# Attention scores with a second level of Strassen's rule in four of seven products, and the next image's block sums at a later place

## The chip, the cores and the metric

The kernel runs on one core of one Trainium2 chip. The metric is device time in microseconds (us) of one execution. Before the change three runs gave 2621.7, 2623.08 and 2623.68 us, median 2623.08. One further execution was taken with the hardware profiler: 2621.26 us, of which 2619.2 us are the span of the trace and 2.06 us lie around it. The clock granted to TensorE was 1.00 of full speed in that execution.

The engines are named as the profile names them: PE (TensorE, matrix products; PEld is its weight load), ACT (ScalarE), DVE (VectorE), POOL (GpSimd), SP (SyncE, which only issues transfers here). PSUM is the memory that PE writes its results to.

## The reference

Two images x of 512 channels and 32 by 32 = 1024 positions go through a deformable attention block with an MLP (layer 0) and then through a plain attention block (layer 1). The change lies in layer 1 alone:

```python
q = xt @ Wq.T + bq          # xt: 1024 positions x 512 channels
k = xt @ Wk.T + bk
v = xt @ Wv.T + bv
attn = softmax(q @ k.T / sqrt(512))
out = (attn @ v) @ Wp.T + bp
return x + out.T
```

Everything is float32. The kernel folds the weights: with G from Wq and Wk, the scores are Q^T x, where Q = G x + bias has 512 channels by 1024 positions (what is constant along a softmax row is left out); and N from Wv and Wp replaces v and the last projection.

## The kernel before, in words

**Layer 1, per image b (the loop at L1192).** All products are multiplied by Strassen's rule (in Winograd's form): a 2 by 2 block matrix product takes seven block products instead of eight, numbered by `PARTS` (L104) with the weight block and the moving block that each takes. Sums of blocks, made by DVE (`fold`, `spread`, `plus`) or POOL, feed the products and combine the results. The stages of one image are, in PE's order:

1. *q stage* (L1224): seven products of G with x give Q in four quadrants `qs[0..3]` of 256 channels by 512 positions; `fold` (L1228) adds the three block sums `qs[4..6]` on DVE.
2. *scores* (`scores(u)`, L1248; u = 0, 1): for 512 query positions at a time, Q^T x against all 1024 positions. Each of the seven products is 256 queries x 512 keys over 256 channels: four `nc.tensor.matmul` calls, which the trace shows as 8 PE passes of 512 columns (two passes to a float32 call). The result quadrants c11, c12 (tile `e[0]`) and c21, c22 (`e[1]`) are filled by ACT copies and DVE additions out of PSUM. `softmax(e[1])` is traced after product 5 and `softmax(e[0])` after product 2, the last: a row maximum (DVE, L1235), a scale of it (L1236), two exponentials (ACT, L1239), a reciprocal (DVE, L1243), two multiplications (ACT, L1245).
3. *turn* (`turn(u)`, L1271): PE transposes the 512 x 1024 result into PSUM in four pieces of 8 passes, ACT copies each to `aT` (L1280), DVE makes two block sums (`spread`).
4. *v products* (`turned`, L1294): seven products of x with N, three of them between turn(0) and turn(1), four after.
5. *value stage* (from L1318): attn times v. Here four of the seven products (1, 6 in set 0; 7, 5 in set 1) are already split by a second level of the rule, by `twice` (L139); products 2, 3, 4 run whole (`plain`).

**`twice` (L139 to L180)** works on pairs of outer products ("sets"). Each set is seven inner steps in the order `STEPS` (L137): q = 1, 2, 6, 5, 7, 4, 3 at times 0, 1, 3, 4, 6, 9, 12; the second set starts 7 later; whole products and other work are slipped in at given times (`fills`). An order written out by hand holds for PE: every step is issued after the newest PE instruction. Steps 1, 6, 7 and 4 of a set pile up in one PSUM bank of a tile, and ACT copies the running sum out after each (lines 166, 170, 172, 176: d11, d12, d22, d21), so step 6 may start only when ACT has copied step 1, and so on. Steps 2, and 5 with 3, go to the two banks of a second tile; DVE adds step 2 to d11, step 5 to d22 and step 3 to d12. The MLP of layer 0 (`layer1`, L1057) uses the same function with inner blocks of 128 x 256 over 128 channels, each step being two calls, 4 passes of 256 columns.

**Order on the other engines.** Dependences and queue order are set by a scheduler at build time: an engine that comes free takes, of what is ready, the instruction that stands first in the program. The queue is then fixed, and each engine executes its own in order. `tc.issue_after` adds an edge behind an instruction of the same engine.

**PSUM** has four buffers of 128 x 1024 for these stages (`mq`, L1150), taken in rotation.

**`blocks(b)` (L925)** makes the three sums t1, t2, t3 (tile `tx`) and t4 of x that the q stage, the scores and the v products take as moving blocks: four DVE instructions, no transfers. For image 1 it is traced inside `second()` (L1416), the fill at time 6.5 of image 0's value stage, after `x_sums(1)` and `w_sums(1)`, and behind the newest DVE instruction.

Of the kernel before, what the change touches and what calls it, by code (L numbers as in the profile page):

```python
# [8 lines left out]
F32 = mybir.dt.float32  # L9
AF = mybir.ActivationFunctionType  # L10
ALU = mybir.AluOpType
# [3 lines left out]
P = 128  # L15
# [42 lines left out]
def conv_seq_kernel(ctx: ExitStack, tc: tile.TileContext, x, xt, kst, pst, cst, vec, wsm, outw, w1, w2, wl, wlt, brow, out):  # L58
    nc = tc.nc
# [52 lines left out]
    PARTS = {1: (0, 0), 2: (1, 2), 3: (6, 3), 4: (2, 6), 5: (4, 4), 6: (5, 5), 7: (3, 1)}  # L112
# [17 lines left out]
    def multiply(pool, order, product, took):  # L130
        for p in order:
            ps = pool.tile([P, 2, 512], F32, tag="ps2", name="sw")
            product(ps, *PARTS[p])
            took[p](ps)

    def plus(out, a, b_, op=ALU.add):
        nc.vector.tensor_tensor(out, a, b_, op)  # L137
# [44 lines left out]
    AT_W, AT_X = ((0, 0), (1, 0), (1, 1), (0, 1)), ((0, 0), (0, 1), (1, 0), (1, 1))  # L182
# [24 lines left out]
    with tc.tile_pool(name="lp", bufs=2) as lp:  # L207
# [37 lines left out]
        def load(b, k, wq=None):  # L245
# [367 lines left out]
        head, g, n = chain(0), weights(0), weights(1)  # L613
# [233 lines left out]
        for s in range(NS):  # L847
# [36 lines left out]
            if bg is None and s > ready and (s - ready) % 4 == 0 and (s - ready) // 4 <= 8:  # L884
                i = (s - ready) // 4 - 1
# [39 lines left out]
    def blocks(b):  # L925
        tx = xq.tile([P, 3, 2, 512], F32, tag="tx", name="tx")
        q = quarters(b)
        t1, t2, t3 = (tx[:, j] for j in range(3))
        t4 = f_pool.tile([P, 2, 512], F32, tag="sx", name="t4")
        nc.vector.tensor_tensor(t1, q[0], q[1], ALU.subtract)  # L930
        nc.vector.scalar_tensor_tensor(t2, t1, -1.0, q[3], ALU.mult, ALU.subtract)
        nc.vector.tensor_tensor(t3, q[3], q[1], ALU.subtract)
        nc.vector.scalar_tensor_tensor(t4, t2, -1.0, q[2], ALU.mult, ALU.subtract)
        return [q[0], t3, q[2], q[3], t1, t2, t4]

    with ExitStack() as top, tc.tile_pool(name="wp", bufs=1) as wp:
        halves = [(b, h) for b in range(B) for h in range(2)]
# [213 lines left out]
        for i, (b, p) in enumerate(units):  # L1151

            j, k = divmod(i, NCH)
# [37 lines left out]
    with tc.tile_pool(name="sp", bufs=1) as sp:  # L1191
        for b in range(B):  # L1192
# [27 lines left out]
            def q5(ps):  # L1220
                plus(q22, q22, ps)
                plus(q12, q12, ps)

            multiply(mq, (1, 6, 7, 4, 5, 3, 2), product(gg, xbl), {  # L1224
                1: q1, 6: lambda ps: plus(q12, q11, ps), 7: q7, 4: lambda ps: plus(q21, q22, ps), 5: q5,
                3: lambda ps: plus(q12, q12, ps), 2: lambda ps: plus(q11, q11, ps),
            })
            fold(nc.vector, [qs[:, j] for j in range(7)], ALU.subtract)  # L1228


            aT = sp.tile([P, 6, 4, 512], F32, name="aT")

            def softmax(e, sign):
                mx = sp.tile([P, 2], F32, name="mx1", bufs=4)
                nc.vector.tensor_reduce(mx, e, AX.X, ALU.max if sign > 0 else ALU.min)  # L1235
                nc.vector.tensor_scalar(mx, mx, -SC * sign, None, ALU.mult)  # L1236
                sm = sp.tile([P, 2], F32, name="sm1", bufs=4)
                for m in range(2):
                    nc.scalar.activation(  # L1239
                        e[:, m, :], e[:, m, :], AF.Exp, bias=mx[:, m : m + 1], scale=SC * sign,  # L1240
                        accum_out=sm[:, m : m + 1],
                    )
                nc.vector.reciprocal(sm, sm)  # L1243
                for m in range(2):
                    nc.scalar.activation(e[:, m, :], e[:, m, :], AF.Copy, scale=sm[:, m : m + 1])  # L1245


            def scores(u):  # L1248
                e = [sp.tile([P, 2, HW], F32, name=f"e{i}", bufs=2) for i in range(2)]
                c11, c12, c21, c22 = (e[i][:, :, n : n + 512] for i in range(2) for n in (0, 512))  # L1250

                def s7(ps):
                    plus(c22, c12, ps)
                    plus(c21, c22, c21, ALU.subtract)

                def s5(ps):
                    plus(c22, c22, ps)
                    plus(c12, c12, ps)
                    softmax(e[1], -1)

                def s2(ps):
                    plus(c11, c11, ps, ALU.subtract)
                    softmax(e[0], 1)

                multiply(mq, (4, 1, 6, 7, 5, 3, 2), product(qs, xbl, 256 * u), {
                    4: lambda ps: nc.scalar.copy(c21, ps), 1: lambda ps: nc.scalar.copy(c11, ps),
                    6: lambda ps: plus(c12, c11, ps), 7: s7, 5: s5, 3: lambda ps: plus(c12, c12, ps), 2: s2,
                })
                return e

            def turn(u, e):  # L1271
                for i in range(2):
                    for m in range(2):
                        ps = mq.tile([P, 2, 512], F32, tag="ps2", name="psx")
                        for c in range(8):
                            nc.tensor.transpose(  # L1276
                                ps[:, c // 4, c % 4 * P : (c % 4 + 1) * P], e[i][:, m, c * P : (c + 1) * P], ident
                            )
                        n = 256 * u + m * P
                        nc.scalar.copy(  # L1280
                            aT[:, i : i + 3 : 2, :, n : n + P],
                            ps.rearrange("p a (c n) -> p a c n", n=P),
                        )
                n = slice(256 * u, 256 * u + 256)
                spread([aT[:, j, :, n] for j in range(6)], range(2))

            e0 = scores(0)
            e1 = scores(1)
            turn(0, e0)
            vt = cp.tile([P, 7, 4, 256], F32, tag="big", name="vt")  # L1290
            vf = [vt[:, j].rearrange("p m n -> p (m n)") for j in range(7)]
# [23 lines left out]
            multiply(mq, (1, 6, 7), turned, took)  # L1315
            turn(1, e1)

            sets = ((1, 6), (7, 5))  # L1318
            where = {p: (g, e) for g, pair in enumerate(sets) for e, p in enumerate(pair)}
# [79 lines left out]
            def plain(p, took):  # L1399
                def go():  # L1400
                    ps = mq.tile([P, 2, 512], F32, tag="ps2", name="sw")
                    whole(ps, *PARTS[p])
                    took(ps)
                return go
# [9 lines left out]
                    spread([aT[:, j] for j in range(6)], (2,))  # L1414

            def second():  # L1416
                nonlocal xbl
                x_sums(1)
                w_sums(1)
                if b + 1 < B:  # L1420
                    with tc.issue_after(newest(mybir.EngineType.DVE)):
                        xbl = blocks(b + 1)
# [2 lines left out]
                (-1, plain(2, lambda ps: plus(x11, x11, ps))),  # L1425
                (-2, third),
                (6.5, second),
                (15, plain(3, lambda ps: plus(x12, x12, ps))),
                (20, plain(4, a4)),
            ), 1.0)  # L1430
# [116 lines left out]
```

## Time and profile before

| what | value |
|---|---|
| median of three runs | 2623.08 us |
| profiled execution, its span | 2621.26 us, 2619.2 us |
| q stage, image 0 / image 1 (PE) | 2313.96 to 2338.00 / 2464.46 to 2488.49 |
| scores(0), scores(1), image 1 | 2488.49 to 2512.53, 2512.53 to 2536.56 (24.04 us each) |
| turn(0), v products, turn(1), image 1 | 2536.56 to 2567.72 |
| value stage, image 0 | 2417.23 to 2464.46 (47.2 us) |
| value stage, image 1 | 2567.72 to 2613.04 (45.3 us) |
| DVE and ACT busy in scores(1), image 1 | 13.30 us and 10.71 us of 24.03 |

Times are read on the axis of the trace, in us from the start of the span. A timeline line gives the start, the length, the engine, the source line, the operation, output and inputs, and in brackets how long the engine was idle before it and what ended the wait. PE passes are pipelined: the length of a PE line includes the drain of its last pass, so the pace is read from one start to the next. L137 is the helper `plus`, L160 the products of `twice`, L1200 the whole products.

### The profile page before, as it was taken

The page shows a single profiled execution, that of the slowest core. Times are in us where ns is not written, and L with a number is a line of the kernel's source. Part 1 is how long each engine was busy: PE and PEld are TensorE (multiplying, and loading weights), DVE is VectorE, ACT ScalarE, POOL GpSimd, SP SyncE. Part 2 cuts the span into 40 slices and gives each one's busy share as a digit, 9 for nine tenths or more (in the row PEclk, how much of TensorE's full clock was granted, in tenths as well). Part 3 has the DMA queues.
Part 4 walks back from the last instruction along what each step waited for, and adds up shares of the span by engine and source line. Part 5 has one row for each costly group of instructions (what it writes and reads, how often), then busy time and mean ns, then how long its engine had stood idle before and what let it go on. Part 6 is the DMA issues. An engine that isn't in the chain of part 4 may idle for free.

```text
span 2619.2 us, 48156 instructions
## 1 busy us (share of the span) xinstructions
PE 2603.7 (99%) x19752; PEld 1030.5 (39%) x19752; DVE 2313.2 (88%) x1463; ACT 1750.4 (67%) x2325; POOL 814.1 (31%) x909
## 2 busy tenths in 40 slices
PE   9999999999999999999999999999999999999999
PEld 3333343333233233333333333334355655646556
DVE  7999999999999999999999999999786586666656
ACT  5887898878888887887887777777733242314041
POOL 1333333333333333333333333333332334200100
PEclk9999999999999999999999999999999999999999
DMA  5888878888887889787887878888777768400202
GB/s 189 178 174 184 184 172 171 183 180 196 173 176 169 180 171 205 172 180 169 181 183 164 182 172 178 173 185 177 147 209 172 150 150 166 87 17 1 73 0 57
DMA packets 167531, 407.74 MB, mean 156 GB/s; under 512 B 24944, under 2 KB 73216, under 8 KB 164624
## 3 DMA queue, kind: packets, MB, share of 16 engines
q0 software_dynamic: 100736, 259.43, 54.6%
q1 hardware_dynamic: 66144, 144.93, 15.8%
q8 instruction: 156, 2.56, 0.4%
q14 instruction: 63, 0.52, 0.1%
q10 hardware_dynamic: 432, 0.31, 0.0%
HBM read 82.15 MB, written 6.55 MB: 34 GB/s over the span
## 4 chain that ended last, share of the span: by engine, by line
PE 91%; DVE 4%; ACT 2%; issue 2%; DMA 1%; DVEq 0%; POOL 0%; ACTq 0%; POOLq 0%; SPq 0%
PE ps L698 63%; PE sw L1041 7%; PE sw L1200 7%; PE sw L160 6%; PE sw L988 2%; PE sw L1298 2%; PE sim L784 1%; PE psg L600 1%; DVE hm L137 1%; PE psx L1276 1%; ACT rx L707 1%; DVE ub L717 0%; DVE h L681 0%; PE pkv L534 0%; DVE oe L137 0%
## 5 line engine op out<-in xcount | busy, mean ns | idle before, releaser
L698 PE MATMUL ps<-h,cw 128*32 128x512 f32 x16384 | 1776.4, 592 | 4.2 <-ACT rx L707 3.1
L681 DVE CUSTOM_DVE_ANT_1 h<-ta,tb 128x4096 f32<-128x4096 f32 (+1 forms) x257 | 1130.9, 4401 | 29.5 <-PE ps L698 26.7
L698 PEld LDWEIGHTS ps<-h,cw 128*32 128x32 f32 x16384 | 549.0, 110 | 1195.8 <-issue 1123.4
L707 ACT ACTIVATE rx<-ps,sc 128x1024 f32<-128x1024 f32 x512 | 568.2, 1110 | 146.6 <-PE ps L698 125.2
L709 ACT ACTIVATE ub<-ps,sc 128x1024 f32<-128x1024 f32 x256 | 308.3, 1204 | 93.2 <-PE ps L698 93.0
L717 DVE SCALAR_TENSOR_TENSOR ub<-rx,sc,ub 128x1024 f32<-128x1024 f32 x256 | 326.8, 1276 | 6.6 <-ACT ub L709 6.6
L736 POOL DMA_DIRECT2D ua<-uc x126 | 154.4, 1235 | 319.5 <-DMA ua<-uc 312.7
L736 POOL DMA_DIRECT2D ua<-ua x189 | 219.4, 1306 | 26.0 <-DMA ua<-uo 19.1
L1041 PE MATMUL sw<-hm,w2t 128*128 128x512 f32 x448 | 193.9, 592 | 0.8 <-DVE hm L125 0.7
L719 POOL DMA_DIRECT2D uo<-ub x127 | 123.7, 974 | 221.7 <-DVE ub L717 207.0
L709 ACT ACTIVATE uo<-ps,sc 128x1024 f32<-128x1024 f32 x128 | 154.2, 1205 | 51.7 <-PE ps L698 51.4
L717 DVE SCALAR_TENSOR_TENSOR uo<-rx,sc,uo 128x1024 f32<-128x1024 f32 x128 | 163.5, 1278 | 8.2 <-ACT uo L709 8.2
L736 POOL DMA_DIRECT2D uc<-uo x63 | 53.1, 842 | 333.7 <-DMA uc<-uo 327.6
L1041 PEld LDWEIGHTS sw<-hm,w2t 128*128 128x128 f32 x448 | 84.9, 190 | 105.3 <-issue 98.2
L137 DVE TENSOR_TENSOR hm<-hm,sw 128x512 f32<-128x512 f32 (+1 forms) x80 | 58.7, 738 | 69.9 <-PE sw L160 50.4
L719 POOL DMA_DIRECT2D ua<-ub x64 | 58.4, 912 | 170.3 <-DVE ub L717 160.5
L661 ACT ACTIVATE ta<-fb,vs 128x512 f32<-128x512 f32 (+1 forms) x65 | 88.9, 1370 | 8.0 <-DMA fb<-fdr 8.0
L709 ACT ACTIVATE ua<-ps,sc 128x1024 f32<-128x1024 f32 x64 | 77.0, 1204 | 20.5 <-PE ps L698 20.1
L709 ACT ACTIVATE uc<-ps,sc 128x1024 f32<-128x1024 f32 x64 | 77.1, 1205 | 20.1 <-PE ps L698 17.7
L1364 POOL DMA_DIRECT2D xs<-rs x6 | 7.2, 1195 | 261.4 <-DVE rs L137 261.4
L166 ACT COPY hm<-sw 128x512 f32<-128x512 f32 x24 | 14.1, 587 | 111.2 <-PE sw L160 111.2
L717 DVE SCALAR_TENSOR_TENSOR uc<-rx,sc,uc 128x1024 f32<-128x1024 f32 x64 | 81.8, 1278 | 2.7 <-ACT uc L709 2.5
(294 smaller groups left out, 2659.5 us busy)
## 6 DMA issues: line engine op xcount, KB each, us to landing
uo<-ub POOLq DMA_DIRECT2D x127, 512.0 KB, 5.6
fb<-fdr SPq DMA_DIRECT2D x64, 512.0 KB, 5.1
ua<-ub POOLq DMA_DIRECT2D x64, 512.0 KB, 5.8
uc<-ub POOLq DMA_DIRECT2D x64, 512.0 KB, 5.2
ua<-ua POOLq DMA_DIRECT2D x63, 256.0 KB, 6.2
ua<-uo SPq DMA_DIRECT2D x63, 256.0 KB, 2.3
ua<-uo POOLq DMA_DIRECT2D x63, 256.0 KB, 6.0
uc<-uc POOLq DMA_DIRECT2D x63, 256.0 KB, 6.9
```

What stands on the lines that cost most here:

```text
L137: nc.vector.tensor_tensor(out, a, b_, op)
L160: nc.tensor.matmul(bank[:, e, :], w, x, start=(q in (1, 2, 5) and e == k == 0), stop=True, skip_group_check=True,)
L661: nc.scalar.activation(ta.rearrange("p j x -> p x j")[:, :, j0:j1], fb[:, 0, :, j0:j1], AF.Identity, bias=col("cb1"), scale=col("w1x"),)
L681: nc.vector._custom_dve(TENSOR_ADD_SAT, out=h1[:, y : y + step].rearrange("p y t x -> p (y t x)"), in0=a.unsqueeze(1).to_broadcast([P, ste ...
L698: nc.tensor.matmul(ps[32 * q : 32 * q + 32, h, :], cw2[:, 32 * z : 32 * z + 32], h1[:, 16 * h : 16 * h + 16, q, :], start=True, stop=True,)
L707: nc.scalar.activation(o, ps, AF.Relu, bias=sc[:, 4 + z : 5 + z])
L709: nc.scalar.activation(o, ps, AF.Relu, bias=sc[:, 4 + z : 5 + z], scale=sc[:, z : z + 1])
L717: nc.vector.scalar_tensor_tensor(r[1], r[0], sc[:, z : z + 1], r[1], ALU.mult, ALU.add)
L719: nc.gpsimd.dma_start(out=sums[s][1], in_=sums[s][3], accum_op=ALU.add)
L736: nc.gpsimd.dma_start(out=out, in_=in_, accum_op=ALU.add)
L1041: nc.tensor.matmul(ps[:, m, :], w[:, a, k, m * P : (m + 1) * P], x[:, b_, k, :], start=(k == 0), stop=(k == 1),)
L1200: nc.tensor.matmul(ps[:, m, :], w[:, a, k, c + m * P : c + (m + 1) * P], x[b_][:, k, :], start=(k == 0), stop=(k == nk - 1),)
```

## The change

It touches four places.

- **scores(u)** is rewritten on top of `twice`: products 1, 6 (set 0) and 7, 5 (set 1) are split into seven inner products each of 128 queries x 256 keys over 128 channels; products 4, 2 and 3 stay whole, as fills at times -1, 14 and 20. Set 0 accumulates straight into c11 and c12 of `e[0]`; set 1 into scratch r7, r5 (`qr`). `done(1)` combines and calls `softmax(e[1])`; product 3, the last, calls `softmax(e[0])`.
- **Sums for the inner products**: eight DVE instructions for the moving side (`qx`), traced before the q stage; four DVE and four POOL instructions for the weight side (`inner_q`), traced between and after the `fold` instructions.
- **A scratch tile `sw_`** of 48 KB per partition takes the place (tag) of `aT`; `aT` itself is taken only after scores(1), so it comes free for turn(0) when the last reader of `sw_` is done.
- **blocks(b+1)** moves from `second` (time 6.5) to a fill of its own at time 14, behind the newest DVE instruction there.

The diff, with all that matters of it:

```diff
-        return [q[0], t3, q[2], q[3], t1, t2, t4]
+        return [q[0], t3, q[2], q[3], t1, t2, t4, tx]
...
+            sets = ((1, 6), (7, 5))
+            where = {p: (g, e) for g, pair in enumerate(sets) for e, p in enumerate(pair)}
+            sw_ = sp.tile([P, 12, 1024], F32, tag="aT", name="sw_")
+            qx = sw_[:, 0:4, :].rearrange("p j (a n) -> p j a n", a=4)
+            qe = [sw_[:, n : n + 2, :].rearrange("p a (j e u n) -> p (a j) e u n", j=2, e=2, u=2) for n in (4, 6)]
+            qr = sw_[:, 8:10, :].rearrange("p e (m n) -> p e m n", m=2)
+            for t, blk in ((xbl[7][:, 0:3], slice(1, 4)), (xbl[0][:, None], slice(0, 1))):
+                x = [t[:, :, k, 256 * n : 256 * n + 256] for k, n in AT_X]
+                f, a, c, d = (qx[:, j, blk] for j in range(4))
+                plus(a, x[1], x[0], ALU.subtract)
+                plus(c, x[3], a, ALU.subtract)
+                plus(f, x[3], x[1], ALU.subtract)
+                plus(d, x[2], c, ALU.subtract)
             multiply(mq, (1, 6, 7, 4, 5, 3, 2), product(gg, xbl), {
...
-            fold(nc.vector, [qs[:, j] for j in range(7)], ALU.subtract)
-            aT = sp.tile([P, 6, 4, 512], F32, name="aT")
+            def inner_q(g):
...
+                engine = (nc.vector, nc.gpsimd)[g]
+                f, a, c, d = (qe[g][:, j] for j in range(4))
+                engine.tensor_tensor(a, w[3], w[2], ALU.add)
+                engine.tensor_tensor(c, a, w[0], ALU.subtract)
+                yield
+                engine.tensor_tensor(f, w[0], w[3], ALU.subtract)
+                engine.tensor_tensor(d, w[1], c, ALU.subtract)
+            first = inner_q(0)
+            for which in ((0, 1), (3,), (2,)):
+                fold(nc.vector, [qs[:, j] for j in range(7)], ALU.subtract, which)
+                next(first, None)
+            for _ in inner_q(1):
+                pass
...
             def scores(u):
...
-                multiply(mq, (4, 1, 6, 7, 5, 3, 2), product(qs, xbl, 256 * u), {
-                    4: lambda ps: nc.scalar.copy(c21, ps), 1: lambda ps: nc.scalar.copy(c11, ps),
-                    6: lambda ps: plus(c12, c11, ps), 7: s7, 5: s5, 3: lambda ps: plus(c12, c12, ps), 2: s2,
-                })
+                def dest(g, m, h):
+                    if g == 0:
+                        return e[0][:, m, :].rearrange("p (e h n) -> p h e n", e=2, h=2)[:, h]
+                    return qr[:, :, m, 256 * h : 256 * h + 256]
+                r7, r5 = (qr[:, i] for i in range(2))
+                def done(g):
+                    if g == 0:
+                        plus(c12, c12, c11)
+                    else:
+                        plus(r7, r7, c12)
+                        plus(c21, r7, c21, ALU.subtract)
+                        plus(c22, r7, r5)
+                        softmax(e[1], -1)
+                        plus(c12, c12, r5)
+                def p3(ps):
                     plus(c12, c12, ps)
+                    softmax(e[0], 1)
+                twice(mq, sets, weights, moving, dest, done, (
+                    (-1, plain(4, lambda ps: nc.scalar.copy(c21, ps))),
+                    (14, plain(2, lambda ps: plus(c11, c11, ps, ALU.subtract))),
+                    (20, plain(3, p3)),
+                ), 1.0)
                 return e
...
             e1 = scores(1)
+            aT = sp.tile([P, 6, 4, 512], F32, name="aT")
             turn(0, e0)
...
             def second():
-                nonlocal xbl
                 x_sums(1)
                 w_sums(1)
+            def next_blocks():
+                nonlocal xbl
                 if b + 1 < B:
                     with tc.issue_after(newest(mybir.EngineType.DVE)):
                         xbl = blocks(b + 1)
...
                 (6.5, second),
+                (14, next_blocks),
```

More of the change, by code (lines that the diff above doesn't have):

```diff
@@ L1227, in conv_seq_kernel @@
             })
-            fold(nc.vector, [qs[:, j] for j in range(7)], ALU.subtract)
-            aT = sp.tile([P, 6, 4, 512], F32, name="aT")
+            def inner_q(g):
+                w = [
+                    qs[:, (slice(0, 6, 5), slice(3, 5))[g], k, :].rearrange("p e (u n c) -> p n e u c", u=2, n=2)[:, n]
+                    for k, n in AT_W
+                ]
+                engine = (nc.vector, nc.gpsimd)[g]
[11 more added lines that the diff above has]
+                pass
             def softmax(e, sign):
@@ L1250, in scores, with plain, go @@
                 c11, c12, c21, c22 = (e[i][:, :, n : n + 512] for i in range(2) for n in (0, 512))
[L1252 to L1257, printed above, removed]
+                one = product(qs, xbl, 256 * u)
+                def plain(p, took):
+                    def go():
+                        ps = mq.tile([P, 2, 512], F32, tag="ps2", name="sw")
+                        one(ps, *PARTS[p])
+                        took(ps)
+                    return go
@@ new lines, in weights, with moving @@
+                def weights(p, j):
+                    g, e_ = where[p]
+                    a = PARTS[p][0]
+                    if j < 3:
+                        k, n = AT_W[j]
+                        n = 256 * u + P * n
+                        return [qs[:, a, k, n : n + P]]
+                    return [qe[g][:, j - 3, e_, u, :]]
+                def moving(p, j):
+                    b_ = PARTS[p][1]
+                    if j in (0, 2, 3):
+                        k, n = AT_X[j]
+                        return [xbl[b_][:, k, 256 * n : 256 * n + 256]]
+                    return [qx[:, max(j - 3, 0), {0: 0, 4: 1, 5: 2, 1: 3}[b_], :]]
@@ L1258, in s5 @@
+                def p3(ps):
                     plus(c12, c12, ps)
-                    softmax(e[1], -1)
-                def s2(ps):
-                    plus(c11, c11, ps, ALU.subtract)
                     softmax(e[0], 1)
-                multiply(mq, (4, 1, 6, 7, 5, 3, 2), product(qs, xbl, 256 * u), {
-                    4: lambda ps: nc.scalar.copy(c21, ps), 1: lambda ps: nc.scalar.copy(c11, ps),
-                    6: lambda ps: plus(c12, c11, ps), 7: s7, 5: s5, 3: lambda ps: plus(c12, c12, ps), 2: s2,
-                })
+                twice(mq, sets, weights, moving, dest, done, (
[3 more added lines that the diff above has]
+                ), 1.0)
@@ L1316, in conv_seq_kernel @@
             turn(1, e1)
-            sets = ((1, 6), (7, 5))
-            where = {p: (g, e) for g, pair in enumerate(sets) for e, p in enumerate(pair)}
             x45 = [sp.tile([P, 2, 2, 2, 256], F32, tag="e0", name="x45", bufs=2) for _ in sets]
```

## The prediction

> **What bounds the kernel now.** I read first the page's busy times (PE 2603.7 of 2619.2 us) and the chain that ended last (PE 91%), then the busy times by stage for image 1, from the q stage to the value stage:
>
> ```profile
> 2464.46:2488.49 24.03, 24.03 (x57) 10.64 (x56) 9.94 (x10) 1.27 (x2) 3.40 (x3) 1.00 0.17 66
> 2488.49:2512.53 24.04, 24.04 (x58) 10.64 (x57) 14.13 (x12) 2.91 (x3) 0.00 (x0) 1.00 0.00 0
> 2512.53:2536.56 24.03, 24.03 (x58) 10.59 (x56) 13.30 (x13) 10.71 (x15) 0.00 (x0) 1.00 0.00 1
> 2536.56:2567.72 31.16, 31.16 (x177) 28.22 (x176) 20.47 (x19) 18.52 (x24) 0.00 (x0) 1.00 0.00 1
> 2567.72:2613.04 45.32, 45.05 (x161) 30.13 (x159) 32.20 (x33) 6.70 (x10) 3.58 (x3) 1.00 0.23 47
> ```
>
> The columns are window, length, then busy time of PE, PEld, DVE, ACT, POOL. In both halves of the scores (lines 2 and 3) PE has no idle time, DVE works 14 of 24 us, and ACT's softmax of the first half falls into the second (10.71 against 2.91). So PE sets the time, and nothing on PE waits: less PE work gains, and any wait that arises costs in full.
>
> **PE work.** A whole product takes 3.434 us (24.04 / 7). The pace of 256-column passes is shown by the MLP's use of `twice`:
>
> ```profile
> 2038.83 2.12 PE L160 MATMUL sw<-xe,w1e 128*128 128x256 f32 x8
> 2040.79 2.75 PE L160 MATMUL sw<-xb,w1x 128*128 128x256 f32 x12
> 2043.38 1.03 PE L160 MATMUL sw<-xe,w1x 128*128 128x256 f32 x4
> ```
>
> Twelve passes in 2043.38 - 2040.79 = 2.59 us: 0.864 us per step of four. A half becomes 3 x 3.434 + 14 x 0.864 = 22.39 us, so 1.65 us less; four halves, **6.6 us less**.
>
> The weight load of one pass lasts 190 ns beside 216 ns of pass, and the two overlap in these rows. [...]
>
> **blocks(1) moved.** Its four instructions now stand before the addition that an inner product waits for. First DVE's timeline, then PE's, both image 0:
>
> ```profile
> 2440.12 1.22 DVE L931 SCALAR_TENSOR_TENSOR tx<-tx,xs 128x1024 f32<-128x1024 f32 x1
> 2441.26 0.68 DVE L137 TENSOR_TENSOR rs<-rs,sw 128x512 f32<-128x512 f32 x1
> ...
> 2455.38 1.22 DVE L137 TENSOR_TENSOR xs<-xs,sw 128x1024 f32<-128x1024 f32 x1 [5.01 <-DMA xs<-rs]
> ```
> ```profile
> 2429.71 1.99 PE L160 MATMUL sw<-x,oe 128*128 128x256 f32 x8 [0.27 <-DVE rs L137]
> ...
> 2441.99 1.99 PE L160 MATMUL sw<-x,oe 128*128 128x256 f32 x8 [1.65 <-DVE rs L137]
> ```
>
> At 2441.99 PE had waited 1.65 us. Image 0's value stage lasts 47.23 us, image 1's, which has no blocks, 45.32: **1.9 us gained**. At time 14 the four land in DVE's idle 5.01 us (4.6 us of work); PE wants them at 2464.46, 9 us later. They issue no transfer and pass no queue but DVE's.
>
> The same rows show a wait that matters below: **inner step 5 of a set starts only after DVE has added step 2** (2441.26 + 0.68 = 2441.94, PE at 2441.99), though they use different banks.
>
> **Added sums.** qx: 4 instructions of 768 elements and 4 of 256. By the pitches of 512 (0.60 us) and 1024 (1.13 us) I take 0.87 and 0.34: 5.3 us with the dependences; ends 2.4 and 6.9 us. Image 1: DVE idles 5.65 us from 2465.94 to 2471.59. Image 0: they follow the MLP's last addition (2321.36), and DVE idles 7.3 us in the four gaps of the q stage; the products wait for a buffer only four products (13.7 us) later. Cost nothing at either end. POOL's four sums: 1.26 to 2.14 us each by its `gn` rows; the third ends 3.8 to 6.4 us after start, against 8.5 us until PE wants it: nothing, and one for one beyond. DVE's weight sums are priced next.
>
> **Waits in the scores.** Per half DVE's work grows from 13.3 to some 16.9 us (six additions of 512 elements on top of seven of 1024 and two maxima) and ACT's from 10.7 to some 14 (eight copies of 512 in place of one of 1024); both fit into 22.4 us, but PE now waits for single ones. Product 4 of scores(0) starts at time 0. DVE's steps are 0.60 us (512 elements), 1.13 (1024) and 2.20 (maximum), with 0.12 more after a dependence; ACT's 0.49 to 0.59 (d copies), 1.15 (exponential), 1.05 (multiplication); PE's result reaches a reader after 0.25. Who goes first, where several are ready, is read here on ACT:
>
> ```profile
> 2519.20 1.14 ACT L1239 ACTIVATE e<-e,mx 128x1024 f32<-128x1024 f32 x1
> 2520.24 0.19 ACT L1239 ACTIVATION_READ_ACCUMULATOR e<-e,mx 128x1 f32 x1
> 2520.33 1.13 ACT L1239 ACTIVATE e<-e,mx 128x1024 f32<-128x1024 f32 x1
> 2521.37 0.19 ACT L1239 ACTIVATION_READ_ACCUMULATOR e<-e,mx 128x1 f32 x1
> 2521.46 0.99 ACT L1266 COPY e<-sw 128x1024 f32<-128x1024 f32 x1
> 2522.36 2.19 ACT L1245 ACTIVATE e<-e,sm 128x1024 f32<-128x1024 f32 x2
> ```
>
> The copy of scores(1)'s product 1 (its PE work ended at 2519.39) stands behind the second exponential of scores(0): the older instruction goes first. Today that is free, since PE has four buffers; after the change PE waits for each such copy.
>
> *First half.* DVE: q11 at 0.25, folds 1.51 and 2.64, a 3.77, f 4.37, c 4.97, fold 5.57, d 6.70, d11 addition 7.30 to 7.99. Step 6 (due 5.16) needs c: 5.81, a wait of 0.65. Step 5 (due 6.67) needs d11: 8.14, 1.47. Then PE runs through to 24.49.
>
> *Second half.* DVE still has, from 21.31, d12, r7, c12, c21, c22, product 3's addition (0.60 + 5 x 1.13 and a dependence), then two maxima from 27.69 to 32.09, two scales. The new d11 addition runs 32.33 to 33.02; step 5, due 30.59, starts at 33.17: **2.58** (and 0.08 ahead of step 6). ACT starts the exponentials at 32.29 and works through six of the softmax's eight instructions until 38.99; d22, whose product ended at 34.89, comes then; step 4, due 36.61, starts at 39.64: **3.02**. ACT's last two multiplications end at 41.58, then set 1's d11: its step 6, due 40.50, starts at 42.23: **1.73**. The half ends at 54.27.
>
> *Turn.* The same tail of DVE follows scores(1). ACT's first copy to `aT`, due 55.4, waits until 56.46 for the last reader of `sw_`; the fourth transposed piece needs product 3's buffer (added at 56.33 to 57.55): **0.82**. scores(1)'s exponentials start at 62.06, its last multiplications at 69.66; turn(1), due 68.94, starts at 70.82, and its second piece waits a little: **2.06**. In the value stage DVE catches up behind 6.87 us of product 2.
>
> Sum of waits per image: 0.65 + 1.47 + 0.08 + 2.58 + 3.02 + 1.73 + 0.82 + 2.06 = 12.41; less 3.30 of work: +9.1 us, two images +18.2. In image 0 the exponential's table load (1.28 us, idle today) delays the exponentials some 0.3. With -1.9: +16.6. From the profiled execution: 2621.26 + 16.6 = 2637.9. The runs shown lie 0.4 to 2.4 us above that execution, so about 1 us is added: **2639 us**.
>
> The largest wait is 3.0 us; the granted clock stayed 1.00 through one of 1.65 us, and I price no clock loss. [...]
>
> **Rivals.**
> 1. *Faster: the d copies and additions pass ahead of the old softmax.* Place: ACT's and DVE's queues in scores(1). For it: ACT has only 14 us of work in 22.4, and an MLP unit (2037.09 to 2059.11, 22.02 us) loses only 0.4 against 21 x 0.864 + 3.434 = 21.58. Against: the ACT rows above. Price: 0.5 us of waits per half and none in the turn, so (1.0 - 3.3) x 2 - 1.9 = -6.5: 2615, or 2616 with the 1 us. It is faster where an image's waits stay under 4.2 us, and measurably so under 1.6.
> 2. *Slower, but half:* the maximum of e[1] goes before the additions of c12 (it misses its turn by 0.1 us), so exponentials start over 2 us earlier and the burst splits. Waits some 8 per image, +4.7 each, -1.9: 2629.
> 3. *About the same:* rival 2's order and no waits in the turn, 5 to 6 per image: 2624.
> 4. *More:* it doesn't do what it says, passes of 256 columns pace above 0.216 us (0.24: +5.4 in all), or POOL's sums come late: 2645 to 2650.
>
> **Chances.** Forecast (2631 to 2645) 0.66, rival 2 (2629 to 2631) 0.09, rival 4 0.05, rival 3 0.10, rival 1 0.10. About 0.2% (5.2 us) is what a measurement can tell from no change; slower is the forecast and rivals 2 and 4, 0.80. The range 2624 to 2647 leaves out rival 1, half of 3 and some of 4.
>
> **What will show it.** Right: passes L160 at 0.216 us; in scores(1) PE idle ahead of steps 5, 4 and 6 of some 2.6, 3.0, 1.7 us, released by DVE `e` and ACT; scores(1) near 30 us against 24.5 for scores(0); the four instructions of blocks(1) in DVE's idle stretch before the x12 addition, and no 1.65 us wait before them. Wrong: d22's copy in ACT's queue ahead of the exponentials, or scores(1) under 25 us.

## The result and the profile after

The changed kernel takes 2651.44 us (median of 4 runs, 2649.88 to 2653.64) against 2622.39 us before (4 runs beside them): ratio 1.0116, interval 1.0104 to 1.0128. It is slower, as forecast, but by 29 us where 16 were forecast, and 4.4 us above the range. The profiled execution took 2653.64 us, its span 2651.9 us, its mean granted clock 0.993.

The busy times by stage, in the columns of the prediction's first fence (window, length, busy PE, PEld, DVE, ACT, POOL, granted clock; the last two are of DMA); first scores(0) and scores(1) of image 0, then the same of image 1:

```profile
2338.80:2369.57 30.77, 24.91 (x82) 16.48 (x81) 20.20 (x19) 5.65 (x9) 7.11 (x4) 0.89 0.00 0
2369.57:2401.86 32.29, 26.03 (x82) 17.02 (x81) 17.20 (x21) 15.64 (x22) 0.00 (x0) 0.84 0.00 1
...
2504.10:2535.83 31.73, 26.62 (x81) 17.40 (x80) 20.19 (x19) 5.65 (x9) 7.04 (x4) 0.84 0.00 1
2535.83:2566.38 30.55, 26.54 (x81) 16.62 (x80) 17.07 (x21) 14.09 (x21) 0.00 (x0) 0.89 0.00 0
```

Length less PE busy is PE's idle time: 5.86, 6.26, 5.11 and 4.01 us in the four halves, none before. And PE busy, 24.9 to 26.6 us, is more than the 22.39 us of passes that were forecast, with a granted clock below 1.00. So two things grew: waits, and the passes themselves.

| stage (us) | before | forecast | after, image 0 / 1 |
|---|---|---|---|
| scores(0) | 24.0 | 24.5 | 30.77 / 31.73 |
| scores(1) | 24.0 | 29.8 | 32.29 / 30.55 |
| turns with v products | 31.2 | 34.0 | 32.90 / 34.05 |
| value stage | 47.23 / 45.32 | 45.3 | 45.31 / 45.32 |

Scores(0) holds most of what was not foreseen. PE's timeline there, image 0 (in brackets the idle time before, and what ended it):

```profile
2346.66 1.10 PE L160 MATMUL sw<-sw__17139 128*128 128x256 f32 x4 [2.54 <-issue]
2351.08 3.78 PE L160 MATMUL sw<-sw__17139 128*128 128x256 f32 x8 [3.32 <-DVE e L137]
2354.65 2.17 PE L160 MATMUL sw<-tx,qs 128*128 128x256 f32 x8
```

The two waits are those of the forecast, ahead of steps 6 and 5, but 2.54 and 3.32 us long instead of 0.65 and 1.47. (The first is put down to "issue"; the sum c that step 6 takes, DVE's L1251, ended at 2346.56.) The eight passes after the second take 3.57 us to the next start; at 0.216 us each they would take 1.73. Three windows of 3.41 us around the second wait show why (clock is the third number from the end):

```profile
2344.97:2348.38 3.41, 1.10 (x4) 0.68 (x4) 3.41 (x2) 0.58 (x1) 3.33 (x3) 1.00 0.00 0
2348.38:2351.79 3.41, 0.71 (x2) 0.62 (x3) 2.64 (x3) 0.00 (x1) 1.50 (x1) 0.50 0.00 0
2351.79:2355.20 3.41, 3.41 (x10) 2.69 (x9) 0.00 (x0) 0.30 (x1) 0.00 (x0) 0.50 0.00 0
```

From 2348.38 to 2355.20 the clock granted to TensorE is half, so the passes behind the second wait run at half pace for 4 us; before and after it is 1.00. And DVE, which PE waits for, is late because its own instructions last long. DVE's timeline, then POOL's:

```profile
2342.53 0.68 DVE L1250 TENSOR_TENSOR sw__17139<-qs 128x512 f32<-128x512 f32 x1
2343.13 1.76 DVE L1253 TENSOR_TENSOR sw__17139<-qs 128x512 f32<-128x512 f32 x1
...
2346.48 2.28 DVE L119 TENSOR_TENSOR qs<-qs 128x1024 f32<-128x1024 f32 x1
2348.68 1.75 DVE L1254 TENSOR_TENSOR sw__17139<-qs,sw__17139 128x512 f32<-128x512 f32 x1
```
```profile
2342.69 1.65 POOL L1250 TENSOR_TENSOR sw__17139<-qs 128x512 f32<-128x512 f32 x1 [9.66 <-DVE qs L119]
...
2347.76 2.12 POOL L1254 TENSOR_TENSOR sw__17139<-qs,sw__17139 128x512 f32<-128x512 f32 x1
```

The first sum starts 0.16 us before POOL does and takes 0.68 us. The next three, of the same size, start while POOL computes its own sums and take 1.75; the fold of 1024 elements takes 2.28 us, where the two before POOL's start took 2.36 together. With the row left out here (L1251, 2344.81, 1.75 us) that is four instructions of 1.07 us more, 4.3 us on the path to the addition that step 5 waits for.

In scores(1) the wait is ACT's. PE, then ACT, image 0:

```profile
2383.28 2.07 PE L160 MATMUL sw<-sw__17139 128*128 128x256 f32 x4 [6.22 <-ACT e L170]
```
```profile
2379.45 2.17 ACT L1276 ACTIVATE e<-e,sm 128x1024 f32<-128x1024 f32 x2
2381.53 1.13 ACT L1270 ACTIVATE e<-e,mx 128x1024 f32<-128x1024 f32 x1
...
2382.66 0.56 ACT L170 COPY e<-sw 128x512 f32<-128x512 f32 x1
```

All four of scores(0)'s exponentials, from 2376.01 on, go before the copy (L170) that PE waits for. It is the forecast's queue, but one wait of 6.22 us ahead of step 7 in place of three of 2.6, 3.0 and 1.7; image 1 has 1.16 ahead of step 7, 2.09 ahead of step 4 and 0.77 ahead of set 1's step 6. The forecast's wait of 2.58 us ahead of step 5 came in neither image: in image 0 DVE made the addition that step 5 waits for at 2375.19, ahead of the second maximum (2375.79) and not behind it.

**Two theories for the 15.7 us that were not forecast** (profiled execution against 2637.9): *clock and POOL*: POOL beside DVE lengthens the waits of scores(0), and the long waits halve the clock for some us. *Rival, the passes*: `twice`'s passes themselves are dearer here than in the MLP, since their operands lie otherwise, and the lower clock is only a companion.

### The profile page after: what moved, and what is told of

Read it like the earlier page. It is cut to its first block, busy times and chain, and to the rows that moved or that the text cites. A ratio compares the mean times of both kernels' runs of the same rounds, so it can differ in the third digit from the quotient of the medians.

```text
span 2651.9 us, 48437 instructions
## 1 busy us (share of the span) xinstructions
PE 2613.7 (99%) x19848; PEld 1038.0 (39%) x19848; DVE 2351.8 (89%) x1511; ACT 1764.2 (67%) x2353; POOL 836.6 (32%) x917
## 3 DMA queue, kind: packets, MB, share of 16 engines
q1 hardware_dynamic: 66144, 144.93, 15.7%
## 4 chain that ended last, share of the span: by engine, by line
PE 89%; DVE 6%; ACT 3%; issue 2%; DMA 0%; DVEq 0%; ACTq 0%
PE ps L698 63%; PE sw L160 8%; PE sw L1041 7%; PE sw L1200 4%; PE sw L988 2%; PE sim L784 1%; PE sw L1363 1%; PE psg L600 1%; DVE hm L137 1%; ACT e L1270 1%; DVE h L681 1%; DVE e L137 1%; DVE ub L717 0%; ACT e L1276 0%; PE pkv L534 0%
## 5 line engine op out<-in xcount | busy, mean ns | idle before, releaser
L681 DVE CUSTOM_DVE_ANT_1 h<-ta,tb 128x4096 f32<-128x4096 f32 (+1 forms) x257 | 1130.5, 4400 | 29.8 <-PE ps L698 26.9
L698 PEld LDWEIGHTS ps<-h,cw 128*32 128x32 f32 x16384 | 531.9, 110 | 1213.0 <-issue 1153.9
L736 POOL DMA_DIRECT2D ua<-uo x63 | 64.2, 1020 | 64.6 <-DMA ua<-uo 57.7
```

The source lines that it names most:

```text
L681: nc.vector._custom_dve(TENSOR_ADD_SAT, out=h1[:, y : y + step].rearrange("p y t x -> p (y t x)"), in0=a.unsqueeze(1).to_broadcast([P, ste ...
L698: nc.tensor.matmul(ps[32 * q : 32 * q + 32, h, :], cw2[:, 32 * z : 32 * z + 32], h1[:, 16 * h : 16 * h + 16, q, :], start=True, stop=True,)
L736: nc.gpsimd.dma_start(out=out, in_=in_, accum_op=ALU.add)
```

## The experiments

**The blocks alone.** The kernel before with `blocks(1)` in a fill at time 14, nothing else:

```diff
             def second():
-                nonlocal xbl
                 x_sums(1)
                 w_sums(1)
+
+            def next_blocks():
+                nonlocal xbl
                 if b + 1 < B:
...
+                (14, next_blocks),
```

> The kernel before with only the move of blocks(1) to time 14. Theory: PE's wait of 1.65 us in image 0's value stage goes and the stage falls from 47.2 to 45.3 us, 1.9 us in all: 2620.5 us where the kernel before takes 2622.4 (ratio 0.9993). Rival: the four sums collide with the x12 addition or come too late for the next q stage, and the time stays within 0.5 us of before.

Measured: 2619.08 us against 2621.07, ratio 0.9991 [0.9983, 1.0]; the value stage of image 0 fell from 47.23 to 45.31 us, no other stage moved by more than 0.02. This term of the forecast (1.9 us) is right, and the part alone is a small gain, at the edge of what can be measured.

**More passes where PE waits.** The changed kernel with passes that compute nothing of use: calls of 256 columns into set 1's tile, which the real products then overwrite, at two places in each half; 12 calls (24 passes) in scores(0), 5 calls in scores(1).

```diff
+                        for _ in range(n):
+                            nc.tensor.matmul(held[1][:, 0, 0:256], qs[:, 0, 0, 0:P], xbl[0][:, 0, 0:256], start=True, stop=True, skip_group_check=True)
...
+                    (2.5, more((5, 0)[u])), (3.5, more((7, 1)[u])), (5.5, more((0, 4)[u])),
```

> The changed kernel with idle stretches of PE filled: in each scores(0) 5 extra calls (10 passes of 256 columns) before step 6 and 7 before step 5 of set 0, in each scores(1) 1 before step 5 and 4 before step 7; their results are overwritten unread. No wait is taken away. Clock theory: passes ran at half pace (granted clock 0.50) only because PE had stood idle; kept busy, it stays at 1.00 in scores(0) and mostly in scores(1), each scores(0) falls by 2 to 4 us (from 30.8 and 31.7 us to about 28), each scores(1) by 2 to 4, 8 to 14 us in all: about 2640 us. Rival: the passes are slow because their operands come late or are shared with DVE and POOL; then extra passes help nothing, and the time stays at 2651 us or rises by up to 2.

Measured: 2647.2 us, ratio 1.0099 [1.0085, 1.0113]. Scores(0) with 24 more passes became 2.00 and 2.96 us *shorter*, with a clock of 1.00:

```profile
2340.52:2369.29 28.77, 28.07 (x105) 19.59 (x104) 20.22 (x19) 5.65 (x9) 7.13 (x4) 1.00 0.00 0
```

No dependence was taken away; only PE's idle time was filled. So the clock theory is shown in scores(0), and the rival falls there: the passes of `twice`, and 24 more beside them, ran at full pace. In scores(1) the filling was too small: waits of 4.36 us in image 0 and of 1.61 and 1.42 in image 1 were left, the clock was 0.94 and 0.89, and the stage changed by -1.60 and +0.65. The whole gained 4.2 us (2.9 when each kernel is set against the runs of the kernel before that were taken beside it), where 8 to 14 were expected.

**POOL later, first try.** Fold 3, which POOL's sums wait for, exchanged with fold 2:

```diff
-            for which in ((0, 1), (3,), (2,)):
+            for which in ((0, 1), (2,), (3,)):
```

> The changed kernel with two fold instructions exchanged, so that fold 3, on which POOL's sums wait, is DVE's last one. Port theory: DVE's sums with two operands from SBUF lasted 1.75 instead of 0.68 us only because POOL worked beside them; now they are 0.68 us, step 5 of set 0 starts some 8 us after product 4 instead of 12.3, PE's idle time in each scores(0) falls from 5 to 6 us to about 2, the clock stays at 1.00 there, and each scores(0) takes 24.5 to 25.5 us instead of 30.8 and 31.7: 2638 to 2640 us. Rival: the sums are slow because of their pattern of access (rows of 128 out of four blocks); then they stay at 1.75 us and scores(0) stays above 30 us.

Measured: 2652.47 us, ratio 1.0119 [1.0103, 1.0134]; scores(0) 30.62 and 31.69. It decides nothing: the order that the scheduler made put fold 3 ahead of the sums all the same (two folds in a row at 2339.60), POOL started at 2342.04 beside DVE's sums, and these took 1.75 us as before.

**The softmax behind scores(1).** Both softmaxes are traced after scores(1), so that its copies go first:

```diff
-                        softmax(e[1], -1)
+                        late.append((u, e[1], -1))
-                    softmax(e[0], 1)
+                    late.append((u, e[0], 1))
...
             e1 = scores(1)
+            for _, e_, sign in late:
+                softmax(e_, sign)
```

> The changed kernel with the softmax of both halves traced after scores(1), so that scores(1)'s copies and additions stand before scores(0)'s softmax in the order of the program. Queue theory: PE's waits of scores(1) come from older softmax work going first; idle time there falls from 6.3 and 4.0 us to 2 to 3, no half clock follows, and scores(1) takes 25 to 26.5 us instead of 32.3 and 30.6; the turn may lose up to 1 us more; 2640 to 2643 us. Rival: ACT and DVE simply have too much work in scores(1), whatever the order: scores(1) stays above 29 us or the loss moves to the turn, and the time stays near 2651 us.

Measured: 2637.77 us, ratio 1.0062 [1.0049, 1.0076], 13.7 us less than the change (12.4 with each set against the runs beside it). Scores(1) of image 1 (image 0 took 23.05 us, with as little idle time and the same clock):

```profile
2528.38:2551.24 22.86, 22.86 (x81) 14.82 (x80) 17.19 (x21) 13.78 (x21) 0.00 (x0) 1.00 0.00 0
```

PE no longer idles, the clock is 1.00, and the turns are what they were in the change (32.91 and 34.05). ACT has as much to do, in another order. The queue of the old softmax is shown to be the whole of scores(1)'s loss. The line also corrects a term: a half without waits takes 22.86 us, not 22.39. In this stage twelve passes go from 2533.61 to 2536.50, 2.89 us in place of 2.59 (2.93 in image 0): short stalls, counted as busy.

**All sums on DVE.** POOL is left out and DVE has four sums more:

```diff
-                engine = (nc.vector, nc.gpsimd)[g]
+                engine = nc.vector
```

> All eight weight sums on DVE, none on POOL. Theory (DVE's instructions with two SBUF operands last about 1.07 us longer while POOL computes beside them): with POOL idle the sums of 512 elements fall from 1.75 to 0.68 us and fold 2 from 2.28 to 1.22 us, although DVE now issues four more of them; scores(0) falls from 30.8 and 31.7 us to 26 to 28 us, with a granted clock of 0.95 or more, and the whole by 4 to 9 us, to 2643 to 2648 us. Rival (the sums are slow by their own shape, strided slices of qs): they stay at 1.75 us, four more of them stand ahead of the d11 addition, the wait at step 5 grows by some 5 us or more, and the whole comes to over 2660 us.

Measured: 2645.78 us, ratio 1.0092 [1.0078, 1.0106]. DVE's second kind of sum, its fold, and what PE then did:

```profile
2343.98 0.69 DVE L1253 TENSOR_TENSOR sw__17139<-qs 128x512 f32<-128x512 f32 x1
...
2345.18 1.22 DVE L119 TENSOR_TENSOR qs<-qs 128x1024 f32<-128x1024 f32 x1
```
```profile
2349.46 3.78 PE L160 MATMUL sw<-sw__17139 128*128 128x256 f32 x8 [2.99 <-DVE e L137]
```

The same instructions on the same operands take 0.68 and 1.22 us once POOL is still, and DVE is done earlier though it does more. That they are slow by their shape is excluded. Scores(0) is 29.12 and 27.97 us, the first a little over the 26 to 28 expected: the three sums that now stand ahead of the addition leave a wait of 2.99 us, and after it the clock is halved again (0.88 in that stage and 0.94 in image 1, where 0.95 or more was expected).

**POOL behind DVE.** The same instructions on the same engines as in the change; fold 3 is held behind DVE's last weight sum:

```diff
-            for which in ((0, 1), (3,), (2,)):
+            for which in ((0, 1), (2,)):
...
+            with tc.issue_after(newest(mybir.EngineType.DVE)):
+                fold(nc.vector, [qs[:, j] for j in range(7)], ALU.subtract, (3,))
```

> Fold 3, which POOL's sums wait for, is held behind DVE's last weight sum, so that POOL starts when DVE has mostly work with a PSUM operand left. Same instructions on the same engines. Theory (POOL beside DVE): DVE's four sums 0.68 us each, fold 2 1.22 us; the waits of scores(0) shrink to 0.5 to 2.5 us, its clock to 1.00, its time to 24.5 to 27 us in both images; the whole 2638 to 2643 us. Rival (the late order of the DVE queue, not its speed): the d11 addition starts no earlier, since fold 3 now stands ahead of it too, scores(0) stays at 30 us or more and the whole at 2650 us.

Measured: 2638.83 us, ratio 1.0066 [1.0051, 1.0082], 12.6 us less than the change (11.6 with each set against the runs beside it). DVE, POOL and PE of image 0, and scores(0) as a whole:

```profile
2344.42 0.69 DVE L1254 TENSOR_TENSOR sw__17139<-qs,sw__17139 128x512 f32<-128x512 f32 x1
...
2346.16 0.68 DVE L137 TENSOR_TENSOR e<-e,sw 128x512 f32<-128x512 f32 x1
2349.55 0.69 DVE L137 TENSOR_TENSOR e<-e,sw 128x512 f32<-128x512 f32 x1 [2.72 <-ACT e L172]
```
```profile
2346.32 1.26 POOL L1250 TENSOR_TENSOR sw__17139<-qs 128x512 f32<-128x512 f32 x1 [13.31 <-DVE qs L119]
...
2348.76 1.27 POOL L1251 TENSOR_TENSOR sw__17139<-sw__17139,qs 128x512 f32<-128x512 f32 x1
```
```profile
2346.89 2.00 PE L160 MATMUL sw<-sw__17139 128*128 128x256 f32 x8 [1.78 <-DVE e L137]
```
```profile
2338.75:2363.36 24.61, 22.83 (x82) 15.06 (x80) 16.02 (x19) 5.64 (x9) 4.99 (x4) 1.00 0.00 0
```

The wait is 1.78 us (1.75 in image 1), the clock stays 1.00, and scores(0) is 24.61 and 24.60 us: the 24.5 of the forecast. DVE's addition at 2349.55, which reads PSUM (`sw`), starts in the middle of POOL's third sum and takes its 0.69 us all the same; POOL's takes 1.27, not 1.65 to 2.12. So what suffered in the change were DVE instructions with both operands in SBUF that start while POOL computes, and POOL's sums with them.

**Put together.** Four further kernels ask whether the split scores can be made to gain. The first leaves scores(0) whole and splits scores(1) alone (its weight sums on DVE, 256 elements each); the second keeps the whole change with both mends. In both, the softmaxes come behind scores(1) and the order of v's products is changed:

```diff
-            turn(0, e0)
...
-            multiply(mq, (1, 6, 7), turned, took)
+            multiply(mq, (1, 6, 7, 5), turned, took)
+            turn(0, e0)
+            multiply(mq, (3,), turned, took)
             turn(1, e1)
...
-            multiply(mq, (5, 3, 4, 2), turned, took)
+            multiply(mq, (4, 2), turned, took)
```

> Scores(0) by the old seven whole products, scores(1) by the new rule (weight sums of its half alone, 256 elements each, all on DVE and done during scores(0)); both softmaxes behind scores(1); v's products run 1, 6, 7, 5, then turn(0), 3, turn(1), 4, 2; the blocks moved as in the change. Theory (the saving of 1.65 us per half is real, and only its preparations and the ACT queue spoil it): scores(0) 24.0 us, scores(1) 22.8 to 23.1, turns with v 31.2 to 32.2, clock 1.00 throughout, value stage 45.3; the whole 2616 to 2620 us, faster than before by 0.1 to 0.25%. Rival (128-column weight loads or 256-column passes cost the half what they save): scores(1) 24 us or more, and the whole no faster than the run with the blocks alone, 2619 to 2622 us.

> The whole change, with POOL held behind DVE's sums, both softmaxes behind scores(1), and v's products reordered around the turns as in the run before. Theory: scores(0) 24.5 to 27 us, scores(1) 22.8 to 23.1, turns with v 31.2 to 32.5 us, clock 1.00; the whole 2618 to 2627 us, no more than 0.2% off the kernel before. Rival (a loss spread over the whole change, such as its extra instructions, apart from the three waits): the whole stays over 2632 us.

Measured: 2623.92 us, ratio 1.001 [1.0001, 1.0019], for the half, where 2616 to 2620 were expected, and 2624.94 us, ratio 1.0014 [1.0005, 1.0023], for the mended whole. For the mended whole, scores(0) 24.60 and 24.60, scores(1) 23.05 and 22.87, turns with v 31.27 and 31.27, as expected: the loss of 29 us shrinks to 3.6. For the half, scores(1) took 23.35 and 23.40 (a wait of 0.44 and 0.48 us for ACT's copy), 0.65 less than whole products take, where 22.8 to 23.1 were expected. But the value stage rose, to 49.45 and 47.77 us in the mended whole and 47.77 and 49.46 in the half, where 45.3 was expected. Turn(1) came two products later, and with it, as the last two kernels test, DVE's sums for the value product. PE in the value stage of the mended whole, image 0 and image 1:

```profile
2427.36 1.97 PE L160 MATMUL sw<-x,oe 128*128 128x256 f32 x8 [0.54 <-DVE oe L137]
2431.28 3.15 PE L160 MATMUL sw<-x,oe 128*128 128x256 f32 x8 [1.95 <-DVE rs L137]
```
```profile
2579.59 1.97 PE L160 MATMUL sw<-x,oe 128*128 128x256 f32 x8 [0.54 <-DVE oe L137]
2583.51 1.99 PE L160 MATMUL sw<-x,oe 128*128 128x256 f32 x8 [1.95 <-DVE rs L137]
```

The waits are alike to the hundredth, and the passes behind them are not (3.15 and 1.99 us): the clock fell in image 0 and not in image 1. PE was busy 46.96 and 45.29 us in these two value stages, so one fall of the clock cost 1.67 us. What the falls go with is taken up below.

The last two kernels put turn(1) only one product later (v's products 1, turn(0), 6, 7, 5, turn(1), 3, 4, 2), first with the whole change mended, then with scores(1) alone:

> As the kernel with all three parts mended, but v's products run 1, turn(0), 6, 7, 5, turn(1), 3, 4, 2: turn(1) stands one product later than before the change, not two. Theory (the value stage lost 2.1 and 4.1 us there because turn(1) came two products later and left DVE's sums for the value product short of time): turns with v 31.2 to 32 us, value stage 45.3 to 46.2, scores as they were (24.6, 23.0); the whole 2618 to 2622 us, between no change and 0.15% faster than before. Rival (the value stage lost it to the softmaxes behind scores(1), whatever the order of v): value stage 47 us or more, the whole 2624 us.

> As the kernel with scores(1) alone by the new rule, with v's products in the order 1, turn(0), 6, 7, 5, turn(1), 3, 4, 2. Theory: scores(0) 24.0, scores(1) 23.4, turns with v 31.2 to 32, value stage 45.3 to 46.2; the whole 2616 to 2620 us, faster than before by 0.05 to 0.2%. Rival (the softmaxes behind scores(1) cost the value stage 2 us or more whatever the order of v): value stage 47 us or more, the whole 2622 to 2624 us.

Measured: 2625.19 us, ratio 1.0014 [1.0005, 1.0022], and 2624.07 us, ratio 1.0009 [1.0, 1.0018]. The value stage came down as expected (46.06 and 45.76 in both), the turns with v went up (33.44 and 33.32 for 31.27; 33.45 and 33.31 in the other). In the mended whole a v product now waits 1.38 us for DVE's addition of the one before it, and busy PE is 0.76 us more (both image 0). The theory was right about the value stage: the later turn(1) was what that stage lost by. It was wrong about the turns, where most of what the value stage gets back is lost again; the rival's total came, but not its value stage of 47 us or more. None of these versions beats the kernel with the blocks alone; that one (2619.08 us) stays the best of the study.

## Why the prediction was wrong

**Right:** the sign; the blocks (1.9 us forecast, 1.92 measured); and that scores(0) waits for DVE and scores(1) for ACT behind the old softmax. The sum of the waits, 24.8 us forecast for scores and turns and 24.7 measured, agrees by luck: scores(0) waited 6.7 us more than forecast in the two images, scores(1) 4.5 less and the turns 2.3 less. Rival 1 needed the copies ahead of the softmax: the fourth experiment makes that case by hand, for scores(1).

**Wrong, the step that failed: "The granted clock stayed 1.00 through one of 1.65 us, and I price no clock loss."** Busy PE in the four halves is 104.1 us. Four halves without waits and at full clock take 4 x 22.86 = 91.4 (fourth experiment). The other 12.7 us are passes at half clock, most of the 15.7 missed. The row of 1.65 us was read rightly: that wait cost no clock, nor did one of 1.78 us (POOL behind DVE, image 0). The mistake was to carry it to forecast waits of 2.6 and 3.0 us, for which no row stood. Of the 12.7 us, 6.9 lie in scores(1), where waits of such a size were forecast; 5.8 lie in scores(0), where they come of the next error.

A shorter wait was followed by a fall as well: in the value stage of the mended whole, image 0, one of 1.95 us, at the cost of the 1.67 us.

**What a fall goes with.** In layer 1 of the changed kernel's trace, up to PE's last product, the changes of the clock lie whole multiples of 3.413 us apart: it falls at 2348.38, 2379.10, 2512.22 and 2549.76 and comes back 2, 3, 3 and 2 such stretches later. In the stretch ahead of each fall PE had idled 2.31, 2.08, 2.58 and 2.08 us; the other stretches at a clock of 1.00 held 1.63 us or less. The stretches lay otherwise in other executions: by these times one would begin at 2426.89 and the next at 2430.30, while the rows below have 2428.54 and 2428.29. The value stage of image 0 with the waits of 0.54 and 1.95 us, first two stretches of the mended whole, then one of the half:

```profile
2428.54:2431.95 3.41, 1.46 (x7) 0.98 (x6) 3.41 (x3) 0.58 (x1) 0.00 (x0) 1.00 0.00 0
2431.95:2435.37 3.42, 3.42 (x10) 2.71 (x9) 3.39 (x4) 0.00 (x0) 0.00 (x0) 0.50 0.02 5
```
```profile
2428.29:2431.70 3.41, 1.60 (x7) 1.44 (x8) 3.38 (x4) 0.48 (x1) 0.00 (x0) 1.00 0.00 0
```

In the first the whole wait of 1.95 us falls into one stretch, and the next one runs at half clock. In the second 1.81 us of it do, and the clock stays at 1.00; so it does in image 1 of the mended whole, where an edge cuts the wait and the two stretches hold 1.12 and 1.37 us of idle time. So in these rows it is the idle time within one stretch that goes with a fall, and not the length of one wait. It is not the whole of it: in the fourth experiment the stretch from 2500.94 held 2.00 us, and the next one ran at 1.00. What sets a fall was not shown, and no run changed it on purpose.

**Wrong, the price of POOL's sums: "nothing, and one for one beyond".** They were looked at for their own end and not for what they do to DVE. Measured: 1.07 us on each of four DVE instructions on the path. Through it scores(0)'s waits were 10.97 us in the two images; with POOL held back 3.52, against 4.24 forecast. What was missed here set off the halved clock as well: holding POOL back took 7.45 us of waits and 5.84 us of busy PE out of scores(0).

The trace of before held a warning, in DVE's additions at the end of the value stage, image 0, then image 1:

```profile
2459.72 4.56 DVE L137 TENSOR_TENSOR xs<-xs,rs 128x1024 f32<-128x1024 f32 x3
```
```profile
2608.31 3.49 DVE L137 TENSOR_TENSOR xs<-xs,rs 128x1024 f32<-128x1024 f32 x3
```

The same three instructions take 1.07 us longer in image 0, where POOL computes its `gn` sums from 2461.94 on, and not in image 1, where it doesn't. POOL's sum from 2463.28, beside the last of the three, takes 2.13 us where the others take 1.26 or 1.27; the prediction's upper price for one sum, 2.14 us, is about this row's.

In the changed kernel DVE's sums of 512 elements beside POOL's start 1.68 and 1.67 us apart (from 2343.13 on), and POOL's 1.61 and 1.67 (from 2342.69 on). Alone, DVE's start 0.60 us apart (all sums on DVE) and POOL's 1.22 (POOL behind DVE), which is 1.82 us together: beside each other the two go nearly at the pace of one behind the other. Why was not shown.

Rival 4 came nearest in time, 2645 to 2650 us, but not for its reason: POOL's own sums were early enough (the last ended at 2349.88 in image 0; PE took them up at 2357.5).

**Smaller errors.** Work of a half: 22.39 forecast, 22.86 measured, 1.9 us over four halves. The prediction's own rows show one of the short stalls: at 2038.83 eight passes take 1.96 us in place of 1.73. Scores(1) waits: 7.4 us an image forecast, 6.26 and 4.01 measured, and for ACT alone. Turns: 5.8 us forecast, 3.4 idle measured. With the clock these add up: busy PE +14.5 (12.7 and 1.9), waits in the scores +2.2, turns by their length -1.1, what lies ahead of the q stage and around the span +0.5 (the start of the q stage alone differs by up to 4.3 us between the profiled executions): 16.1 us, less the 0.3 us of the table load that the forecast had besides its waits: the 15.7 missed.

**Open:** why the one stretch with 2.00 us of idle time was followed by none at half clock, and whether an order of turns and v products exists in which the split scores gain.

## What to carry to other kernels

This kernel, whose PE did not idle in the scores before, paid twice for its new waits: 21.2 us of idle time in the four halves, and 12.7 us of passes at half clock. Four stretches of 3.41 us in the changed kernel and one in the mended whole, with 1.95 to 2.58 us of idle time each, were followed by a half clock, one with 2.00 us (fourth experiment) was not; the loss was 1.7 to 3.8 us in a value stage or in a half of the scores. Where forecast waits come to as much, price that loss too. Before a sum goes to POOL "for nothing", look at what DVE does at that time: if both its operands lie in SBUF, each such instruction cost 1.07 us more here, nearly as much as POOL's own sum (1.26). And look at the stages behind: in the mended whole 1.0 us was saved in the scores, and 6.6 us were lost in the value stage against the 45.3 us that it takes without the late turn; with turn(1) earlier, 4.4 us in the turns and 1.2 in the value stage.

## What the runs showed of the hardware

**Waits and the granted clock.** In layer 1 of the changed kernel's trace, up to PE's last product, the clock fell to 0.50 four times, each time behind a stretch of 3.413 us with 2.08 to 2.58 us of PE idle time; behind stretches at 1.00 with 1.63 us or less it stayed at 1.00. At half clock the stretches held 2.70 and 0.00 us of idle time, then 3.41, 0.76 and 0.00, then 1.78, 0.75 and 0.00, then 0.77 and 0.00: each time the clock came back behind the one with 0.00. Single waits of 1.65 us (before the change), 1.63 (the changed kernel, 2583.01), and 1.78 and 1.75 (POOL behind DVE) left the clock at 1.00. In the changed kernel the clock was 0.50 at the end of the waits of 3.32, 6.22 and 2.54 us, at 2351.08, 2383.28 and 2516.38, and fell 1.72 and 0.22 us behind the end of those of 2.54 and 2.58 us, at 2346.66 and 2512.00. Waits of 1.61 and 1.42 us went with a clock of 0.89 in their stage (more passes, scores(1) of image 1), and waits of 0.54 and 1.95 us, the passes behind them 3.92 us apart, with a fall in image 0 of the mended whole and with none in its image 1. The 1.95 us in image 0, and a wait of 2.09 us in the changed kernel (to 2549.42), each lay whole within one stretch, and a fall followed.

**POOL beside DVE.** Sums of DVE with two SBUF operands: 512 elements 0.68 to 0.69 us without POOL (all sums on DVE), 1.74 to 1.76 beside its sums (the changed kernel); 1024 elements 1.22 and 2.28. POOL's sum of 512: 1.26 to 1.27 us alone (POOL behind DVE), 1.58 to 2.12 beside DVE's (the changed kernel). A DVE addition of 512 elements that reads PSUM: 0.67 to 0.69 us either way (49 of them start while POOL computes a sum of 512, in the traces of before and of the changed kernel).
